# Messages of a graph layer as fp32 rows, with the edges' loop codes as one more column of the product

## The chip, the cores and the metric

The kernel runs on one core of a Trainium2 chip. The metric is the device time of one execution, in microseconds, as the median of several runs. PE is the matmul engine, DVE the vector engine, ACT the scalar engine, POOL and SP the engines that mostly issue DMAs here.

## The reference

A graph has 6,250 nodes with 256 features and 106,250 edges, sorted by destination; each node also has edges to itself (loops). Two layers follow one another, each with a residual and a layer norm. The first one has this core:

```
def edge_nn(x, W, b):
    h = relu(x @ W.T + b)
    return relu(h @ W.T + b)
msgs = zeros
for r in range(2):                       # two kinds of edges
    msgs = where((rel == r)[:, None], edge_nn(feat[src], W_rel[r], b_rel[r]), msgs)
agg = segment_sum(msgs, dst)
gates = agg @ W_ih.T + b_ih + b_hh       # i, f, g, o
c = sigmoid(i) * tanh(g);  hn = sigmoid(o) * tanh(c)
x = relu(hn @ W1.T + b1);  x = relu(x @ W2.T + b2);  return x @ W3.T + b3
```

The second one is a graph attention layer with 4 heads over the same edges: a softmax over the edges that arrive at a node, and a sum of the source rows weighted by it.

## The kernel before

**The start** (`gnn_kernel`, up to L1170). Since a message depends only on the source node and the edge's kind, all 2 x 6,250 messages are computed once per node. For chunks of 4 blocks of 128 nodes, PE makes the hidden layer (`fph`, L1135), ACT its relu (`fhT`, L1142), PE the messages of a block (`fpm`, L1149, a PSUM tile of two buffers). DVE adds the bias (L1158, into `fms`) and ACT takes the relu (L1161). The fp32 message is then split into three bf16 numbers that add up to it, with two ACT casts (L1162, L1164) and two DVE subtractions (L1163, L1165) into `ms3`, and SP stores a block of 384 KB to the table `parts0` in DRAM (L1167): one row of 3 x 256 bf16, 1,536 bytes, for each node and kind.

In the same stretch the chip looks at the edge list. Loops are taken out and the list is compacted: a ladder of shifts on DVE (L885 to L903, into `frame`), 21 indirect scatters by POOL into `packed` (L932), reads back by SP (`both`, L962), then integer work on DVE that gives for each edge its row in `parts0`, its destination, and `mark`, a code that is not zero at the one edge of a node which carries its loops' kinds. The per-edge lists are turned on PE (L1060) so that 128 edges lie on the partitions: 782 tiles of 128 edges. `low_p` (L1077) is PE's first product that needs the list. The order of instructions in this stretch is set by a scheduler, and every engine then runs its queue in order.

**Layer 0** (`fast`). The order is written out by hand, as a loop over the tiles in which `run.step()` advances generators by one step a tile. A group is 14 tiles, whose edges end in at most 128 nodes. For each tile POOL gathers 128 rows of `parts0` (`gather`, L1262) into a buffer `G`, a ring of 10 with 4 tiles each. Four tiles later PE adds the tile to the group's sum with a one-hot matrix of destinations as the weights (`oh0`, made by DVE at L1346 from `iota_s`): a product of 512 columns (L1631, the two upper parts side by side), one of 256 (L1632, the third part), and one of a single column (L1633), which carries `mark` into `codes`, a column of the PSUM tile `bank`. The group's sum `fps0` has two buffers.

When a group is complete, `turn` finishes it: ACT copies the code (L1436), DVE makes two selection matrices from it (`pick`, L1439), PE adds the nodes' own rows `loop0` with four products (L1445, L1446), ACT and DVE fold the two halves (L1450, L1452), PE transposes (L1456) and DVE copies into `faT` (L1459). `update` then takes up to four groups through the gates (L1483) and the small dense layers to `hr` (L1570), the rows of the second layer's table `rows1`. The last groups are taken one at a time; the last of all stores its rows with a POOL scatter (L1579), and only then can the second layer's gathers begin.

**Layer 1** gathers 782 tiles again, from `rows1` (1,040 bytes a row, same helper, same ring, 7 tiles a buffer), weights them on DVE (L1811) and sums them with fp32 products (L1920).

Of the kernel before, what the change touches and what calls it, by code (L numbers as in the profile page):

```python
# [30 lines left out]
F32 = mybir.dt.float32  # L35
I32 = mybir.dt.int32
AF = mybir.ActivationFunctionType
OP = mybir.AluOpType
# [5 lines left out]
P = 128  # L44
N = 6250
D = 256
E = 106250
H = 4
# [6 lines left out]
ZERO0 = 2 * NP  # L55
# [10 lines left out]
BF16 = mybir.dt.bfloat16  # L66
WT = 7
TC = -(-(E - N) // P)
NW = -(-TC // WT)
SLOTS = 64  # L70
NG = NW // 2
CT = 18 * WT
# [4 lines left out]
HA = D + H  # L77
# [627 lines left out]
def gnn_kernel(  # L705
# [26 lines left out]
    nc = tc.nc  # L732
# [6 lines left out]
        return at(ap, 0, [[0, P], [1, n]])  # L739

    dram = ctx.enter_context(tc.tile_pool(name="fdram", bufs=1, space=DRAM))
    parts0 = dram.tile([ZERO0 + 1, 3 * D], BF16, name="parts0")
    rows1 = dram.tile([NP + P, HA], F32, name="rows1")
    slots = dram.tile([NW, (WT + 1) * P], BF16, name="slots")
    cuts = dram.tile([(NC + 1) * CT, P], F32, name="cuts")
# [27 lines left out]
    with (  # L773
# [8 lines left out]
        with nc.allow_non_contiguous_dma(reason="bias vectors, one element a partition"):  # L782
            nc.scalar.dma_start(brc, br.rearrange("r (k p) -> p r k", p=P))
        nc.scalar.dma_start(brr, rows(br, 2 * D))
        zrow = mw.tile([1, 3 * D], BF16, name="fzrow")
        nc.vector.memset(zrow, 0.0)
        nc.sync.dma_start(parts0[ZERO0 : ZERO0 + 1, :], zrow)

        with (
# [260 lines left out]
            for to, of in (  # L1050
                (idx0, row),
                (dstE, list_f[:, :, 1:]),
                (mark, rel_f[:, :, :P]),
                (idx1, src0),
                (first, steps),
            ):
                for k0, kn in blocks_of(NC, 4):
                    pt = lps.tile([P, 4 * CT], F32, name="turned")
                    for k in range(kn):
                        nc.tensor.transpose(  # L1060
                            pt[:, k * CT : (k + 1) * CT], of[:CT, k0 + k, :], ident[:CT, :CT]
                        )
                    n = min(kn * CT, COLS - k0 * CT)
                    nc.vector.tensor_copy(to[:, k0 * CT : k0 * CT + n], pt[:, :n])
            ones = lp.tile([P, P], F32, name="fones")
            nc.vector.memset(ones, 1.0)
            few = lps.tile([P, 4 * CT], F32, name="turned")
# [56 lines left out]
        for b0, bn in blocks_of(NB, CHUNK):  # L1124
            cols = bn * P
            xc = mp.tile([P, 2, CHUNK * P], F32, name="fxc", bufs=3)
            nc.sync.dma_start(
                xc[:, :, :cols], xT[:, b0 * P : b0 * P + cols].rearrange("(k p) n -> p k n", p=P)
            )
            hT = mp.tile([P, 2, 2, CHUNK * P], F32, name="fhT")  # L1130
            for r in range(2):
                for m in range(2):
                    ph = mps.tile([P, CHUNK * P], F32, name="fph")
                    for k in range(2):
                        nc.tensor.matmul(  # L1135
                            ph[:, :cols],
                            WrT_s[:, r, k, m * P : (m + 1) * P],
                            xc[:, k, :cols],
                            start=(k == 0),
                            stop=(k == 1),  # L1140
                        )
                    nc.scalar.activation(  # L1142
                        hT[:, r, m, :cols], ph[:, :cols], AF.Relu, bias=brc[:, r, m : m + 1]
                    )
            for j in range(bn):
                pm = mps.tile([P, 2, D], F32, name="fpm")
                for r in range(2):
                    for k in range(2):
                        nc.tensor.matmul(  # L1149
                            pm[:, r, :],  # L1150
                            hT[:, r, k, j * P : (j + 1) * P],
                            WrT_s[:, r, k, :],
                            start=(k == 0),
                            stop=(k == 1),
                        )
                ms = mp.tile([P, 2, D], F32, name="fms", bufs=3)
                ms3 = mp.tile([P, 2, 3, D], BF16, name="ms3", bufs=3)
                nc.vector.tensor_add(  # L1158
                    ms.rearrange("p r f -> p (r f)"), pm.rearrange("p r f -> p (r f)"), brr
                )  # L1160
                nc.scalar.activation(ms, ms, AF.Relu)  # L1161
                nc.scalar.copy(ms3[:, :, 0, :], ms)  # L1162
                nc.vector.tensor_sub(ms, ms, ms3[:, :, 0, :])  # L1163
                nc.scalar.copy(ms3[:, :, 1, :], ms)  # L1164
                nc.vector.tensor_sub(ms3[:, :, 2, :], ms, ms3[:, :, 1, :])  # L1165
                b = b0 + j
                nc.sync.dma_start(  # L1167
                    parts0[2 * b * P : 2 * (b + 1) * P, :].rearrange("(p r) f -> p (r f)", r=2),
                    ms3.rearrange("p r c f -> p (r c f)"),
                )  # L1170

    odd_v = nc.values_load_multi_w_load_instructions(
# [20 lines left out]
def fast(  # L1193
# [111 lines left out]
    GS = 2 * WT + 1  # L1305
    loops = parts0[: 2 * NP, :].rearrange("(n r) f -> n (r f)", r=2)
    iops = ctx.enter_context(tc.tile_pool(name="iops", bufs=1, space=PSUM))
    bank = iops.tile([P, SLOTS + 4 * GS * H + NG], F32, name="bank")
    iota_s = bank[:, :SLOTS]
    exs = bank[:, SLOTS : SLOTS + 4 * GS * H].rearrange("p (b t h) -> p b t h", b=2, h=H)  # L1310
    codes = bank[:, SLOTS + 4 * GS * H :]
    nc.scalar.copy(iota_s, iota_f[:, :SLOTS])
    keep = ctx.enter_context(tc.tile_pool(name="keep", bufs=1))

# [44 lines left out]
    with (  # L1359
# [37 lines left out]
            zero[: (NP + P - N) // 2, : 2 * HA],  # L1397
        )

        kinds = l0w.tile([P, 2, P], BF16, name="kinds")  # L1400
        for r in range(2):
            nc.vector.tensor_scalar(
                kinds[:, r, :], ident, float(4 - r), 1.0, op0=OP.mult, op1=OP.subtract
            )

        run = Steps()

        def weights_of_logits():
# [21 lines left out]

        def turn(g, i, ps, aT):

            u = everyone
            agg = ring(up, [P, D], F32, "agg", 2)
            code = ring(up, [P, 1], F32, "code", 3)
            nc.scalar.copy(code, codes[:, g : g + 1])  # L1436
            pick = ring(up, [P, 2, P], BF16, "pick", 2)
            for r in range(2):
                nc.vector.tensor_scalar(  # L1439
                    pick[:, r, :], kinds[:, r, :], code, None, op0=OP.is_equal  # L1440
                )
            yield 1
            for r in range(2):
                own = loop0[g][:, 3 * D * r : 3 * D * (r + 1)]
                nc.tensor.matmul(ps, pick[:, r, :], own[:, : 2 * D], start=False, stop=False)  # L1445
                nc.tensor.matmul(  # L1446
                    ps[:, :D], pick[:, r, :], own[:, 2 * D :], start=False, stop=(r == 1)
                )
            yield 1
            nc.scalar.copy(agg[u, :], ps[u, D:])  # L1450
            yield 1
            nc.vector.tensor_add(agg[u, :], agg[u, :], ps[u, :D])  # L1452
            yield 1
            pt = ring(upp, [P, 4 * P], F32, "fpg", 5)[:, : 2 * P]
            for k in range(2):
                nc.tensor.transpose(  # L1456
                    pt[:, k * P : (k + 1) * P], agg[:, k * P : (k + 1) * P], ident
                )
            nc.vector.tensor_copy(  # L1459
                aT[:, :, i * P : (i + 1) * P], pt.rearrange("p (k n) -> p k n", k=2)  # L1460
            )
# [156 lines left out]
        def sum0(g, t, last=False):  # L1618
# [6 lines left out]
                ohj = ohs[g][:, ohj, :]  # L1625
            begins = g not in sums
            if begins:
                sums[g] = ring(eps, [P, 2 * D], F32, "fps0", 2)
            part = got[t]
            ends = last or j == WT - 1  # L1630
            nc.tensor.matmul(sums[g][to, :], ohj, part[:, : 2 * D], start=begins, stop=False)  # L1631
            nc.tensor.matmul(sums[g][to, :D], ohj, part[:, 2 * D :], start=False, stop=False)  # L1632
            nc.tensor.matmul(  # L1633
                codes[to, g : g + 1], ohj, mark[:, t : t + 1], start=begins, stop=ends
            )
            if last:
                quad = next(q for q in quads if g in q)
                if g == quad[0]:
# [7 lines left out]
        for n in range(TC + LAG):  # L1646
            if n < TC:
                g, t = order[n]
                k = n % 4
                if k == 0:  # L1650
                    four = ring(rowsp, [P, WT * HA], F32, "G", 10)[:, : 6 * D]
                    four = four.bitcast(BF16).rearrange("p (j f) -> p j f", j=4)

                got[t] = four[:, 3 - k if n // 40 % 2 else k, :]
                gather(got[t], parts0, idx0[:, t : t + 1])
                if t == order_of(g)[0]:
                    ohs[g] = ring(ep, [P, 2 * W8, SLOTS], BF16, "oh0", 3)
                    one_hot(ohs[g], 2 * g, 2 * W8)
                    loop0[g] = ring(up, [P, 6 * D], BF16, "loop0", 2)
                    own_rows(g, lows_of(windows_of(g)), loop0[g], loops)  # L1660
            if n >= LAG:
                g, t = order[n - LAG]
                if t != 2 * WT * g:
                    sum0(g, t, t == TC - 1)
                elif g:
                    sum0(g - 1, t, True)
                if t == 2 * WT * g + WT:
                    sum0(g, 2 * WT * g)
            run.step()
# [361 lines left out]
```

## Time and profile before

| | us |
|---|---|
| median of 3 runs (2313.48 to 2318.78) | 2316.77 |
| the profiled execution's own time | 2315.23 |
| its span on the core | 2313.5 |
| first gather of layer 0 starts | 231.4 |
| last gather of layer 0 starts | 1219.6 |
| first gather of layer 1 starts | 1261.5 |
| last gather of layer 1 starts | 2246.2 |

| engine | busy us | share of the span |
|---|---|---|
| PE | 1524.3 | 66% |
| DVE | 1276.5 | 55% |
| ACT | 570.3 | 25% |
| POOL | 1529.7 | 66% |

No engine is near 100% over the whole, so the shares alone don't say what sets the time; they are means over stretches with different loads. In the groups of the profile, "busy" is followed by the mean duration of one instruction, and after the bar by the idle time of the engine just before these instructions and what ended most of it. A record of an fp32 matmul is half of one call in the source: the profile shows two for each.

### The profile page before, as it was taken

The numbers are of one execution on the slowest core, as the hardware profiler recorded it, in microseconds if no ns is written. First come the engines' busy times: TensorE is split into PE (matmuls) and PEld (weight loads), VectorE is DVE, ScalarE is ACT, GpSimd is POOL, SyncE is SP. The second block draws the span as 40 slices with busy tenths as digits, with TensorE's granted clock in tenths as the row PEclk, the third lists the DMA queues.
The fourth block names the chain that finished last, engine by engine and source line by source line (L and its number), as shares of the span: only waits on it lengthen the run. The fifth ranks groups of instructions, "written<-read, shape, count | busy, mean of one in ns | idle before, by whom it ended". The sixth has DMA issues, their size and how long they took to land. (4 is left out here: it accounts for less than half of the span.)

```text
span 2313.5 us, 24182 instructions
## 1 busy us (share of the span) xinstructions
PE 1524.3 (66%) x6783; PEld 837.2 (36%) x6783; DVE 1276.5 (55%) x3370; ACT 570.3 (25%) x1623; POOL 1529.7 (66%) x1603
## 2 busy tenths in 40 slices
PE   7888587888887788878985245545455355454554
PEld 4646333443444444444453122223223222232322
DVE  7867222333333333233433377777777778777786
ACT  3647012222222222222343021121211211111211
POOL 1110777777777777777772777777777777777760
PEclk9889588899898999988997667667676676666776
DMA  4333867777877778777873455555555555555550
GB/s 141 135 117 148 221 188 214 209 214 212 230 221 209 212 204 227 223 214 208 228 230 95 133 150 154 148 152 156 148 155 150 148 160 144 156 151 152 150 144 25
DMA packets 175914, 397.68 MB, mean 172 GB/s; under 512 B 42451, under 2 KB 74290, under 8 KB 175769
## 3 DMA queue, kind: packets, MB, share of 16 engines
q0 software_dynamic: 88480, 259.38, 41.8%
q1 hardware_dynamic: 64736, 96.55, 13.1%
q10 hardware_dynamic: 22553, 40.12, 5.7%
q8 instruction: 55, 0.90, 0.2%
q14 instruction: 90, 0.74, 0.1%
HBM read 337.38 MB, written 58.55 MB: 171 GB/s over the span
## 5 line engine op out<-in xcount | busy, mean ns | idle before, releaser
L1262 POOL DMA_INDIRECT G<-parts,fidx x782 | 749.2, 958 | 323.8 <-issue 191.3
L1262 POOL DMA_INDIRECT G<-rows,fidx x782 | 747.7, 956 | 240.2 <-issue 222.7
L1920 PE MATMUL fps<-gw,oh 128*64 128x264 f32 (+1 forms) x1674 | 435.8, 471 | 233.6 <-DVE gw L1811 233.6
L1631 PE MATMUL fps<-G,oh 128*64 128x512 bf16 (+1 forms) x837 | 339.8, 425 | 141.3 <-DMA G<-parts,fidx 126.0
L1920 PEld LDWEIGHTS fps<-gw,oh 128*64 128x64 f32 (+1 forms) x1674 | 229.5, 168 | 409.3 <-DVE gw L1811 248.5
L1811 DVE TENSOR_TENSOR gw<-G,bank 128x1792 f32<-128x1792 f32 (+1 forms) x167 | 249.0, 1491 | 178.5 <-ACT gw L1810 177.7
L1632 PE MATMUL fps<-G,oh 128*64 128x256 bf16 (+1 forms) x837 | 239.5, 295 | 0.0
L1346 DVE TENSOR_TENSOR oh<-bank,fslot 128x1024 bf16<-128x1024 f32 (+1 forms) x112 | 136.6, 1220 | 138.6 <-PE bank L1633 136.2
L1483 PE MATMUL fpg<-faT,fWihT 128*128 128x512 f32 (+2 forms) x432 | 175.5, 533 | 12.1 <-DVE faT L1459 12.1
L1439 DVE TENSOR_SCALAR pick<-kinds,code 128x128 bf16<-128x128 bf16 x112 | 25.2, 281 | 274.8 <-ACT code L1436 274.8
L1633 PE MATMUL bank<-fmark,oh 128*64 128x1 bf16 (+1 forms) x837 | 139.7, 172 | 37.5 <-DVE oh L1346 26.3
L1759 PE MATMUL turn<-fident,e 128*120 128x128 f32 (+2 forms) x30 | 13.7, 457 | 223.3 <-ACT e L1953 223.3
L1631 PEld LDWEIGHTS <-oh 128*64 128x64 bf16 (+1 forms) x837 | 90.1, 113 | 190.2 <-issue 178.1
L1632 PEld LDWEIGHTS <-oh 128*64 128x64 bf16 (+1 forms) x837 | 92.8, 114 | 143.1 <-issue 140.7
L1633 PEld LDWEIGHTS <-oh 128*64 128x64 bf16 (+1 forms) x837 | 96.5, 119 | 105.5 <-issue 33.4
L1860 ACT ACTIVATE frs<-fmv,eps_c 128x1 f32<-128x1 f32 x112 | 33.0, 295 | 302.5 <-DVE fmv L1859 151.8
L1149 PE MATMUL fpm<-fWrT,fhT 128*128 128x256 f32 x392 | 97.3, 405 | 14.4 <-DVE fms L1158 14.4
L1135 PE MATMUL fph<-fxc,fWrT 128*128 128x512 f32 (+1 forms) x208 | 94.2, 599 | 8.1 <-DMA fWrT<-in_WrT_dram 6.5
L932 POOL DMA_INDIRECT packed<-frame,place x21 | 22.8, 1085 | 116.0 <-DVE fms L1163 79.1
L1483 PEld LDWEIGHTS fpg<-faT,fWihT 128*128 128x128 f32 x432 | 72.5, 198 | 72.1 <-issue 48.5
L1866 ACT ACTIVATE fy<-fy,frs 128x256 f32<-128x256 f32 x112 | 67.2, 600 | 100.4 <-DVE gw L1805 53.2
L1149 PEld LDWEIGHTS fpm<-fWrT,fhT 128*128 128x128 f32 x392 | 78.9, 205 | 34.5 <-DVE fms L1158 18.4
(249 smaller groups left out, 2123.0 us busy)
## 6 DMA issues: line engine op xcount, KB each, us to landing
kept<-keep SPq DMA_DIRECT2D x56, 384.0 KB
k<-kept ACTq DMA_DIRECT2D x56, 384.0 KB
loop<-parts SPq DMA_DIRECT2D x110, 192.0 KB
parts<-ms SPq DMA_DIRECT2D x49, 384.0 KB
dB<-slots ACTq DMA_DIRECT2D x112, 128.0 KB
G<-parts,fidx POOLq DMA_INDIRECT x782
G<-rows,fidx POOLq DMA_INDIRECT x782
rows<-hr SPq DMA_DIRECT2D x110, 65.0 KB
```

Source lines behind the costliest of these rows:

```text
L1135: nc.tensor.matmul(ph[:, :cols], WrT_s[:, r, k, m * P : (m + 1) * P], xc[:, k, :cols], start=(k == 0), stop=(k == 1),)
L1149: nc.tensor.matmul(pm[:, r, :], hT[:, r, k, j * P : (j + 1) * P], WrT_s[:, r, k, :], start=(k == 0), stop=(k == 1),)
L1262: nc.gpsimd.indirect_dma_start(out=to_tile, out_offset=None, in_=table, in_offset=bass.IndirectOffsetOnAxis(ap=idx, axis=0),)
L1346: nc.vector.tensor_tensor(to[:, :nj, :], iota_s[:, None, :].to_broadcast([P, nj, SLOTS]), of[:, :, None].to_broadcast([P, nj, SLOTS]), op= ...
L1483: nc.tensor.matmul(pg[:, :cols], WihT_s[:, k, c * P : (c + 1) * P], aT[:, k, :cols], start=(k == 0), stop=(k == 1),)
L1631: nc.tensor.matmul(sums[g][to, :], ohj, part[:, : 2 * D], start=begins, stop=False)
L1632: nc.tensor.matmul(sums[g][to, :D], ohj, part[:, 2 * D :], start=False, stop=False)
L1633: nc.tensor.matmul(codes[to, g : g + 1], ohj, mark[:, t : t + 1], start=begins, stop=ends)
L1811: nc.vector.tensor_mul(gw[:, :, :D].rearrange("p j (h f) -> p j h f", h=H), of[:, :n, :D].rearrange("p j (h f) -> p j h f", h=H), ex[:, o ...
L1860: nc.scalar.activation(r, mv[u, k, 1:2], AF.Ln, bias=eps_c[u])
L1866: nc.scalar.activation(y, y, AF.Identity, bias=m, scale=r)
L1920: nc.tensor.matmul(sums[g][to, :], ohj, gw, start=begins, stop=ends)
```

## The change

The three-part bf16 rows become plain fp32 rows: `parts0` holds 256 fp32 a row (1,024 bytes), the casts and subtractions are gone, and a block's store is 256 KB. In layer 0 a tile is summed by one fp32 product of 257 columns. Its last column is `mark`, which ACT copies into the buffer beside the gathered rows, for 7 tiles at once; for this `mark` is kept in the order of the gathers. `G` holds 7 tiles a buffer, `oh0` is fp32 with two buffers, and `codes` is gone. The own rows are added in `turn` by DVE, with two compares and two multiply-adds.

```
-    parts0 = dram.tile([ZERO0 + 1, 3 * D], BF16, name="parts0")
+    parts0 = dram.tile([ZERO0 + 1, D], F32, name="parts0")
...
-                    nc.vector.tensor_copy(to[:, k0 * CT : k0 * CT + n], pt[:, :n])
+                    if to is not mark:
+                        nc.vector.tensor_copy(to[:, k0 * CT : k0 * CT + n], pt[:, :n])
+                        continue
+
+                    to2, of2 = (
+                        ap.rearrange("p (g j) -> p g j", j=2 * WT)
+                        for ap in (mark[:, k0 * CT : k0 * CT + n], pt[:, :n])
+                    )
+                    for a, b, c in ((0, 1, 0), (1, 2, WT), (2, WT + 1, 1), (WT + 1, 2 * WT, WT + 1)):
+                        nc.vector.tensor_copy(to2[:, :, a:b], of2[:, :, c : c + b - a])
...
                 ms = mp.tile([P, 2, D], F32, name="fms", bufs=3)
-                ms3 = mp.tile([P, 2, 3, D], BF16, name="ms3", bufs=3)
...
                 nc.scalar.activation(ms, ms, AF.Relu)
-                nc.scalar.copy(ms3[:, :, 0, :], ms)
-                nc.vector.tensor_sub(ms, ms, ms3[:, :, 0, :])
-                nc.scalar.copy(ms3[:, :, 1, :], ms)
-                nc.vector.tensor_sub(ms3[:, :, 2, :], ms, ms3[:, :, 1, :])
                 b = b0 + j
                 nc.sync.dma_start(
                     parts0[2 * b * P : 2 * (b + 1) * P, :].rearrange("(p r) f -> p (r f)", r=2),
-                    ms3.rearrange("p r c f -> p (r c f)"),
+                    ms.rearrange("p r f -> p (r f)"),
                 )
...
-    bank = iops.tile([P, SLOTS + 4 * GS * H + NG], F32, name="bank")
+    bank = iops.tile([P, SLOTS + 4 * GS * H], F32, name="bank")
...
-        kinds = l0w.tile([P, 2, P], BF16, name="kinds")
-        for r in range(2):
-            nc.vector.tensor_scalar(
-                kinds[:, r, :], ident, float(4 - r), 1.0, op0=OP.mult, op1=OP.subtract
-            )
...
         def turn(g, i, ps, aT):
-            u = everyone
-            agg = ring(up, [P, D], F32, "agg", 2)
-            code = ring(up, [P, 1], F32, "code", 3)
-            nc.scalar.copy(code, codes[:, g : g + 1])
-            pick = ring(up, [P, 2, P], BF16, "pick", 2)
+            agg = ring(up, [P, D], F32, "agg", 3)
+            kind = ring(up, [P, 2], F32, "kind", 3)
             for r in range(2):
                 nc.vector.tensor_scalar(
-                    pick[:, r, :], kinds[:, r, :], code, None, op0=OP.is_equal
-                )
-            yield 1
-            for r in range(2):
-                own = loop0[g][:, 3 * D * r : 3 * D * (r + 1)]
-                nc.tensor.matmul(ps, pick[:, r, :], own[:, : 2 * D], start=False, stop=False)
-                nc.tensor.matmul(
-                    ps[:, :D], pick[:, r, :], own[:, 2 * D :], start=False, stop=(r == 1)
-                )
-            yield 1
-            nc.scalar.copy(agg[u, :], ps[u, D:])
-            yield 1
-            nc.vector.tensor_add(agg[u, :], agg[u, :], ps[u, :D])
+                    kind[:, r : r + 1], ps[:, D:], float(3 - r), None, op0=OP.is_equal
+                )
+            for r, of in ((0, ps[:, :D]), (1, agg)):
+                nc.vector.scalar_tensor_tensor(
+                    agg,
+                    loop0[g][:, r * D : (r + 1) * D],
+                    kind[:, r : r + 1],
+                    of,
+                    op0=OP.mult,
+                    op1=OP.add,
+                )
             yield 1
...
             if begins:
-                sums[g] = ring(eps, [P, 2 * D], F32, "fps0", 2)
-            part = got[t]
-            ends = last or j == WT - 1
-            nc.tensor.matmul(sums[g][to, :], ohj, part[:, : 2 * D], start=begins, stop=False)
-            nc.tensor.matmul(sums[g][to, :D], ohj, part[:, 2 * D :], start=False, stop=False)
-            nc.tensor.matmul(
-                codes[to, g : g + 1], ohj, mark[:, t : t + 1], start=begins, stop=ends
-            )
+                sums[g] = ring(eps, [P, D + 1], F32, "fps0", 2)
+            ends = last or j in (WT - 1, TC - 1 - 2 * WT * g)
+            nc.tensor.matmul(sums[g][to, :], ohj, got[t], start=begins, stop=ends)
...
-                k = n % 4
+                k, turns = n % WT, n // WT // 10 % 2
                 if k == 0:
-                    four = ring(rowsp, [P, WT * HA], F32, "G", 10)[:, : 6 * D]
-                    four = four.bitcast(BF16).rearrange("p (j f) -> p j f", j=4)
-
-                got[t] = four[:, 3 - k if n // 40 % 2 else k, :]
-                gather(got[t], parts0, idx0[:, t : t + 1])
+                    seven = ring(rowsp, [P, WT * HA], F32, "G", 10).rearrange(
+                        "p (j f) -> p j f", f=HA
+                    )
+                    m = min(WT, TC - n)
+                    of, to = mark[:, n : n + m, None], seven[:, :, D : D + 1]
+                    nc.scalar.copy(to[:, ::-1, :][:, :m, :] if turns else to[:, :m, :], of)
+
+                got[t] = seven[:, WT - 1 - k if turns else k, : D + 1]
+                gather(got[t][:, :D], parts0, idx0[:, t : t + 1])
                 if t == order_of(g)[0]:
-                    ohs[g] = ring(ep, [P, 2 * W8, SLOTS], BF16, "oh0", 3)
+                    ohs[g] = ring(ep, [P, 2 * W8, SLOTS], F32, "oh0", 2)
                     one_hot(ohs[g], 2 * g, 2 * W8)
-                    loop0[g] = ring(up, [P, 6 * D], BF16, "loop0", 2)
+                    loop0[g] = ring(up, [P, 2 * D], F32, "loop0", 2)
```

More of the change, by code (lines that the diff above doesn't have):

```diff
@@ L784, in gnn_kernel @@
         nc.scalar.dma_start(brr, rows(br, 2 * D))
-        zrow = mw.tile([1, 3 * D], BF16, name="fzrow")
+        zrow = mw.tile([1, D], F32, name="fzrow")
         nc.vector.memset(zrow, 0.0)
@@ L1307, in fast @@
     iops = ctx.enter_context(tc.tile_pool(name="iops", bufs=1, space=PSUM))
-    bank = iops.tile([P, SLOTS + 4 * GS * H + NG], F32, name="bank")
+    bank = iops.tile([P, SLOTS + 4 * GS * H], F32, name="bank")
     iota_s = bank[:, :SLOTS]
-    exs = bank[:, SLOTS : SLOTS + 4 * GS * H].rearrange("p (b t h) -> p b t h", b=2, h=H)
-    codes = bank[:, SLOTS + 4 * GS * H :]
+    exs = bank[:, SLOTS:].rearrange("p (b t h) -> p b t h", b=2, h=H)
     nc.scalar.copy(iota_s, iota_f[:, :SLOTS])
```

## The prediction

> **What bounds the kernel now.** I read the windows by stage first, then the instructions of the gather helper L1262, then the timeline of the first 232 us. The windows (length; busy us and count of PE, PEld, DVE, ACT, POOL; clock; DMA share; GB/s):
>
> ```profile
> 0.00:231.40 231.40, 191.11 (x646) 123.62 (x646) 169.81 (x276) 121.26 (x209) 28.96 (x36) 0.92 0.40 135
> 231.40:1219.60 988.20, 795.60 (x3705) 410.37 (x3706) 339.35 (x1113) 235.17 (x580) 749.23 (x783) 0.89 0.77 216
> 1219.60:1261.50 41.90, 27.19 (x130) 18.77 (x129) 13.81 (x60) 20.35 (x49) 2.85 (x3) 0.75 0.20 65
> 1261.50:2246.20 984.70, 481.77 (x2198) 270.34 (x2198) 709.28 (x1801) 180.34 (x739) 746.76 (x782) 0.68 0.55 150
> 2246.20:2313.50 67.30, 28.64 (x106) 14.12 (x104) 44.26 (x122) 13.17 (x48) 1.92 (x2) 0.69 0.13 37
> ```
>
> Layer 0 (second) and layer 1 (fourth) take the same 988 and 985 us with quite different PE, DVE and DMA loads. What they share is POOL:
>
> ```profile
> L1262 POOL DMA_INDIRECT G<-parts,fidx x782: 942/946/1402, 231.4 to 1219.6; - x196
> L1262 POOL DMA_INDIRECT G<-rows,fidx x782: 942/946/1218, 1261.5 to 2246.2; - x196
> ```
>
> Each layer issues 782 gathers, each 0.946 us by the median and 0.30 us of issue after it: 1.25 us a gather, 782 x 1.26 = 985. The rows are 1,536 bytes in layer 0 and 1,040 in layer 1 and the median is equal, so bytes don't set it, nor does PE. Time can only go or come where POOL isn't gathering: before 231.4, between 1219.6 and 1261.5, and after 2246.2, which the change doesn't touch.
>
> In the start, PE (191 of 231 us) waits for two things:
>
> ```profile
> PE fpm L1149 <- DVE fms L1158: 14.4, 4, 6.3
> PE low_p L1077 <- DVE low L981: 10.1, 1, 10.1
> ```
>
> The second ends a chain: the list's compaction on DVE (last step L903), 21 scatters on POOL (L932), the reads back (L962), `low`:
>
> ```profile
> 83.84 1.08 DVE L903 TENSOR_TENSOR frame<-frame,moved 128x896 int32<-128x896 int32 x1
> ...
> 144.56 0.98 POOL L932 DMA_INDIRECT packed<-frame,place  x1 [1.51 <-DMA packed<-frame,place]
> ...
> 156.11 0.77 PE L1077 MATMUL low_p<-low,fones 1*128 1x113 f32 x2 [10.08 <-DVE low L981]
> ```
>
> PE then has 67.5 us of work to 223.6, and the last block ends so:
>
> ```profile
> 223.67 0.69 DVE L1158 TENSOR_TENSOR fms<-fpm,fbrr 128x512 f32<-128x512 f32 x1 [0.61 <-PE fpm L1149]
> 224.28 0.68 DVE L1165 TENSOR_TENSOR ms<-fms,ms 128x512 bf16<-128x512 f32 x1
> 224.39 0.63 ACT L1161 ACTIVATE fms<-fms 128x512 f32<-128x512 f32 x1 [0.68 <-DVE fms L1158]
> 225.05 0.62 ACT L1162 CAST ms<-fms 128x512 bf16<-128x512 f32 x1
> 225.70 0.69 DVE L1163 TENSOR_TENSOR fms<-fms,ms 128x512 f32<-128x512 f32 x1 [0.75 <-ACT ms L1162]
> 226.43 0.62 ACT L1164 CAST ms<-fms 128x512 bf16<-128x512 f32 x1 [0.76 <-DVE fms L1163]
> 227.08 0.69 DVE L1165 TENSOR_TENSOR ms<-fms,ms 128x512 bf16<-128x512 f32 x1 [0.68 <-ACT ms L1164]
> ```
>
> Its store and POOL's waits take the 3.6 us to the first gather at 231.36.
>
> [...] the trace has 684 (L1158) and 0.42 us (L1452)[...] in layer 1, 12 fp32 products of 264 columns issue back to back in 5.33 us, 0.444 each, and one tile's three bf16 products (769 columns) are 0.36 apart (starts 1216.39, 1216.75, 1217.11). [...] the column above goes from 0.89 to 0.68 where PE is busy half the time.
>
> **The change, part by part.**
>
> *Splits of the messages (49 blocks).* Gone: 98 DVE subtractions and 98 ACT casts, 67 and 60 us busy; a subtraction takes 0.60 us of DVE's queue (start to start). In this part the scheduler fixes each engine's order when the program is built. Counting DVE's instructions to L903: before, 11 adds L1158 and 20 subtractions; in the changed program's order, 17 adds and no subtraction. That is 20 x 0.60 - 6 x 0.60 = 8.4, plus an idle 0.7: L903 ends **9.1 us earlier**, at 76.7. I went through the adds: PE has each block ready in time, since with fewer DVE instructions between the adds its two PSUM buffers come free. The scatters (61 us) and the reads (9.2) follow unchanged, so `low` comes at 147.
>
> *PE's order.* The scheduler now puts 74 products L1135 and 144 L1149 (source calls; each is two records) ahead of `low_p`, where it had 66 and 128. At 0.86 and 0.4355 us (16 records in 7.03, 32 in 7.07) the moved 8 and 16 are 6.9 + 7.0 = **13.9 us** that go from after `low` to before it. There is room: the earlier part had 15.5 us of idle and 8 us of slow L1149 bursts while DVE was behind. PE's work to `low_p` is 74 x 0.86 + 144 x 0.4355 = 126.4 from 6.5, with 3 for the cold start: about 136, so it still waits 11 us, which absorbs errors here.
>
> *The last block* loses casts and subtractions: 225.02 to 227.77, **2.75 us**. *mark in gather order*: 8 small copies for 2 on DVE after the reads, **+0.5**, on PE's way to the next transposes.
>
> Added wait: `fms` is now what is stored, so an add waits until the store of three blocks ago has landed; behind it in DVE's queue is the compaction. Add 0.7, activation 0.7, issue 0.4, landing some 2.5 (227.77 to 230.4 at the end) are 4.3; three blocks of PE are 5.2. Cost 0, at worst a microsecond in a few places (+5). SP's queue keeps stores, loads of `fxc` and the reads back in the same sequence. Stores and gathers move a third less; nothing waits for those bytes.
>
> First gather: 231.4 - 9.1 - 13.9 - 2.75 + 0.5 = **206.1**.
>
> *Layer 0's sums.* Per product 0.36 becomes 0.44 for 257 columns; x837: +70 us of PE. The four loop products a group (L1445, L1446: some 0.7) go: -40. In their place two 128x1 compares (0.16 each) and two multiply-adds (0.42) on DVE, 1.2 a group, for two `pick` (0.56) and an add (0.42); ACT loses two copies. The transposes now stand one product after the group's last sum, so PE waits some 1.2 us for DVE there, the next group's products behind it; before it waited 1.75 at L1483 for `faT`. ACT gains 112 column copies at some 0.2 (as L1961) = 22 us of 988; PE's first product of seven waits for one that was queued 4 gathers before. The gathers get no wait on ACT, and their waits on PE (102 for 209) are on tiles 70 back. `oh0` in fp32 with two buffers: still 1.22 from PSUM, and its 136 us of waiting for L1633 go. All this is under POOL's 988 us, at **0**: PE would be busy 795.6 - 301 (837 x 0.36) - 40 + 372 (837 x 0.444) = 827 of 988. If that cover fails, see the rivals.
>
> *End of layer 0.* The last sum ends at 1232.6; `code`, `pick`, four products, copy, add, transposes and `faT` run to 1238.04, 5.4 us. The new chain is 0.3 + 0.85 + 0.65 + 0.4, with hand-overs 2.6: **-2.8**, bounds 0 (the previous group's chain on ACT is then last) and -7 (the backlog of 11 products at 1219.6 drains sooner without the `bank` waits). Layer 1 is as before, shifted.
>
> **Sum.** -25.2 - 2.8 = -28.0. The profiled execution took 2315.23 (span 2313.5), so 2287.2; the median of the runs was 1.5 above it: **2288.5**.
>
> **Rivals.** *(a) The start keeps its length in part*: the adds wait for stores or PE, so L903 isn't earlier (2298), or DVE's work after the reads, not PE, paces what follows, and the 13.9 is lost as well (2311). For it: DVE is full from 18 to 85 us. Against: its instructions there fall by 14. Chance 0.20, a quarter of it within 0.2%. *(b) Slower: PE becomes layer 0's bound.* 827 us are at a clock of 0.89; at layer 1's 0.68 they are 827 x 0.89/0.68 = 1082, 94 over POOL's 988: 2382. It decides from a clock under 0.745. For it: fp32 products in layer 1 ran at 0.68. Against: there they come in bursts behind DVE, here one every 1.25 us, and a PE that falls behind is a busy one. 0.07. *(c) The bytes do matter* and a gather gets shorter: 0.01, unbounded below; the equal medians speak against it. *(d) No effect at all*, if PE's work alone sets the start: 2316.8; the waits shown speak against it (inside (a)).
>
> **Numbers.** The main case has 0.72: 2288.5, its own range 2279 to 2297. With the better part of (a) and the bounds above, 2277 to 2305. A measurement tells about 0.2% (4.6 us) from no change. Faster 0.88, same 0.05, slower 0.07.
>
> **What would show it.** First gather near 206; L932's first near 77; `low_p` waiting about 11 us at 147; no wait of `fpm` products on the adds over 2 us before that; gathers at 0.946 and 1.25 apart with 988 us; PE clock of layer 0 above 0.8; 38 to 40 us between the layers. A first gather after 220, or gathers further apart than 1.27, would prove it wrong.

## The result, and the profile after

The kernel after takes **2276.5 us** (median of 4 runs, 2273.88 to 2276.94) against 2316.03 for the kernel before beside it (4 runs): a ratio of 0.9827, with a 95% interval of 0.9810 to 0.9844. The profiled execution of after took 2273.88 us, with a span of 2271.7. The time lies 12 us under the forecast and 0.5 us under the low end of the range. Ratios, here and below, compare fast runs with fast runs and need not equal the quotient of the two medians in the last digits.

The windows of the kernel after, cut at the same events as before (length; busy us and count of PE, PEld, DVE, ACT, POOL; clock; DMA share; GB/s):

```profile
0.00:203.70 203.70, 181.13 (x646) 118.63 (x646) 110.79 (x184) 68.84 (x121) 26.98 (x35) 0.97 0.38 122
203.70:1190.40 986.70, 838.64 (x2702) 353.93 (x2703) 361.53 (x1177) 229.06 (x581) 748.48 (x783) 0.93 0.54 157
1190.40:1221.00 30.60, 16.49 (x75) 10.95 (x73) 11.13 (x50) 15.20 (x38) 2.92 (x4) 0.78 0.19 65
1221.00:2205.10 984.10, 484.51 (x2198) 271.61 (x2198) 708.83 (x1804) 180.86 (x739) 746.23 (x781) 0.68 0.55 151
2205.10:2271.70 66.60, 29.57 (x104) 14.56 (x104) 43.23 (x119) 12.94 (x47) 2.06 (x2) 0.65 0.13 37
```

| stretch | before | after | change | forecast |
|---|---|---|---|---|
| start, to the first gather of layer 0 | 231.4 | 203.7 | -27.7 | -25.2 |
| gathers of layer 0, first to last start | 988.2 | 986.7 | -1.5 | 0 |
| gap, to the first gather of layer 1 | 41.9 | 30.6 | **-11.3** | **-2.8** |
| gathers of layer 1 | 984.7 | 984.1 | -0.6 | 0 |
| end | 67.3 | 66.6 | -0.7 | 0 |

Three stretches came as worked out. The start is within 2.5 us. The two long stretches don't move, though PE has 43 us more to do in layer 0 and a third of the gathered bytes is gone (the DMA share falls from 0.77 to 0.54). The gap is where the forecast failed. What a gather costs is the same in the gathers' lines of after:

```profile
L1265 POOL DMA_INDIRECT G<-parts,fidx x782: 942/946/1431, 203.7 to 1190.4; - x196
L1265 POOL DMA_INDIRECT G<-rows,fidx x782: 942/946/1207, 1221.0 to 2205.1; - x196
```

The timeline of after around the gap (start, us, engine, line, tiles; in brackets the idle time before, and who ended it):

```profile
1190.38 0.95 POOL L1265 DMA_INDIRECT G<-parts,fidx  x1 [0.30 <-issue]
...
1193.23 1.26 PE L1622 MATMUL fps<-G,oh 128*64 128x257 f32 x4
...
1194.53 0.22 DVE L1433 TENSOR_SCALAR kind<-fps 128x1 f32<-128x1 f32 x2 [1.71 <-PE fps L1622]
...
1220.96 0.96 POOL L1265 DMA_INDIRECT G<-rows,fidx  x1 [2.69 <-issue]
```

The last sum of layer 0 ends at 1194.49, 4.1 us after the last gather starts; in the kernel before it ended at 1232.65, 13.1 us after. That is -9.0. From the last sum to the first gather of layer 1 the two take 28.8 and 26.5: -2.3 (parts are cut to tenths so that they add up to the table's). So the shorter chain behind the last sum, for which I forecast -2.8, is right, and what I missed is **the backlog**: the sums that PE still owes when the gathers are done.

What made PE late is seen in its waits. When PE has caught up with POOL, it waits for the next gathered rows. In the kernel before it does that for the last time at 1085.1, ahead of the 720th of the 837 calls in which layer 0's gathered rows are summed; from there on it is behind. Its six largest waits from that call to the end of the last sum (who waited <- for whom: us in total, times, longest):

```profile
PE fpg L1483 <- DVE faT L1459: 5.1, 6, 1.5
PE fps L1445 <- DVE pick L1439: 4.3, 1, 4.3
PE bank L1633 <- ACT code L1436: 2.9, 7, 1.3
PE fpg L1507 <- DVE fhn L1503: 2.4, 2, 1.2
PE fps L1631 <- DMA G<-parts,fidx: 2.4, 1, 2.4
PE bank L1633 <- DVE oh L1346: 1.8, 2, 1.6
```

All waits of the kernel after, from the same call (1055.7) to the end of the last sum:

```profile
PE fps L1622 <- DMA G<-parts,fidx: 4.8, 4, 2.5
PE fpg L1499 <- DVE fhn L1495: 1.8, 2, 1.0
PE fpg L1448 <- DVE agg L1437: 1.3, 2, 0.7
PE fpg L1545 <- DVE keep L1536: 0.3, 1, 0.3
```

The wait for rows in the first list, and 0.2 us of that in the second, lie ahead of the call. From its start, before needs 147.5 us to the end of the last sum: 129.9 of work and 17.4 of waits for DVE and ACT. After needs 138.8: 130.7 of work, 3.4 of waits for DVE, and 4.5 of waits for rows. The last gather starts 134.4 and 134.7 us after that call. So PE's own work is the same within a microsecond (the sums are dearer, the loop products are gone), and 14.0 us of waits for other engines are gone. PE catches up with the gathers again, so not all of the 14.0 is won: the backlog is 9.0 shorter, and 4.5 become waits for rows.

### The profile page after: what moved, and what is told of

The parts are those of the page before. It is cut to its first block, busy times and chain, and to the rows that moved or that the text cites. A ratio compares the mean times of both kernels' runs of the same rounds, so it can differ in the third digit from the quotient of the medians.

```text
span 2271.7 us, 22029 instructions
## 1 busy us (share of the span) xinstructions
PE 1550.3 (68%) x5722; PEld 769.7 (34%) x5722; DVE 1235.5 (54%) x3332; ACT 506.9 (22%) x1525; POOL 1526.7 (67%) x1603
## 5 line engine op out<-in xcount | busy, mean ns | idle before, releaser
L1265 POOL DMA_INDIRECT G<-parts,fidx x782 | 748.5, 957 | 305.7 <-issue 218.4
L1622 PE MATMUL fps<-G,oh 128*64 128x257 f32 (+1 forms) x1674 | 523.4, 425 | 149.2 <-DMA G<-parts,fidx 142.4
L1622 PEld LDWEIGHTS fps<-G,oh 128*64 128x64 f32 (+1 forms) x1674 | 191.9, 147 | 457.4 <-DMA G<-parts,fidx 241.5
L1433 DVE TENSOR_SCALAR kind<-fps 128x1 f32<-128x1 f32 x112 | 12.5, 152 | 308.5 <-PE fps L1622 308.5
L1348 DVE TENSOR_TENSOR oh<-bank,fslot 128x1024 f32<-128x1024 f32 x112 | 135.9, 1213 | 2.2 <-ACT bank L1781 2.2
L1583 DVE COPY nd<-hr 128x4 f32<-128x4 f32 x56 | 10.9, 194 | 162.6 <-ACT hr L1562 162.6
L1157 PE MATMUL fpm<-fWrT,fhT 128*128 128x256 f32 x392 | 89.0, 380 | 0.6 <-DVE fms L1165 0.5
L1750 PEld LDWEIGHTS turn<-fident,e 128*120 128x120 f32 (+2 forms) x30 | 5.0, 168 | 238.0 <-ACT e L1944 236.0
L1801 ACT COPY gw<-bank 128x28 f32<-128x28 f32 (+1 forms) x167 | 28.4, 170 | 228.5 <-DMA dB<-slots 101.3
L1157 PEld LDWEIGHTS fpm<-fWrT,fhT 128*128 128x128 f32 x392 | 73.3, 190 | 17.7 <-issue 5.0
L1165 DVE TENSOR_TENSOR fms<-fpm,fbrr 128x512 f32<-128x512 f32 x49 | 33.6, 687 | 76.1 <-PE fpm L1157 74.9
```

What stands on the lines that cost most here:

```text
L1157: nc.tensor.matmul(pm[:, r, :], hT[:, r, k, j * P : (j + 1) * P], WrT_s[:, r, k, :], start=(k == 0), stop=(k == 1),)
L1165: nc.vector.tensor_add(ms.rearrange("p r f -> p (r f)"), pm.rearrange("p r f -> p (r f)"), brr)
L1265: nc.gpsimd.indirect_dma_start(out=to_tile, out_offset=None, in_=table, in_offset=bass.IndirectOffsetOnAxis(ap=idx, axis=0),)
L1348: nc.vector.tensor_tensor(to[:, :nj, :], iota_s[:, None, :].to_broadcast([P, nj, SLOTS]), of[:, :, None].to_broadcast([P, nj, SLOTS]), op= ...
L1622: nc.tensor.matmul(sums[g][to, :], ohj, got[t], start=begins, stop=ends)
L1801: nc.scalar.copy(gw[:, :, D:HA], ex[:, o : o + n, :])
```

## The experiments

Theory 1: the PSUM tile `bank` is the cause. DVE's comparison (L1346) reads the slot numbers in it while PE writes `codes` into it for every tile (L1633); each waits for the other (in layer 0 of before DVE 136.2 us for L1633, PE 26.3 us for L1346). Theory 2: `turn` is, whose four steps come so late that its transposes stand next to the gates. Theory 3: the number of PE's products is. Beside these, the working of the start was to be tested. Where lines are given, those of a kernel with an edit may be shifted by a few from the kernel that it comes from.

The first four kernels ran on another chip, on which the kernel before takes 3087.3 us: in the profile there of the kernel with the slot numbers in SBUF (below), the gathers of layer 0 stand 1.57 us and those of layer 1 1.89 us apart in the mean, and such stalls hide the gap. From these, only the start, which ends before the gathers, can be read.

**The splits put back into the start of after, into a scratch tile.**

```
                 nc.scalar.activation(ms, ms, AF.Relu)
+                ms3 = mp.tile([P, 2, 3, D], BF16, name="ms3", bufs=3)
+                nc.scalar.copy(ms3[:, :, 0, :], ms)
+                nc.vector.tensor_sub(ms3[:, :, 1, :], ms, ms3[:, :, 0, :])
+                nc.scalar.copy(ms3[:, :, 2, :], ms3[:, :, 1, :])
+                nc.vector.tensor_sub(ms3[:, :, 0, :], ms3[:, :, 1, :], ms3[:, :, 2, :])
```

> The kernel after, with two casts on ACT and two subtractions on DVE of 128x512 put back for each of the 49 blocks, into a scratch tile that nothing reads; the store still waits for the activation alone. My theory of the start (the subtractions stand in DVE's queue ahead of the list's compaction, and the built order then puts fewer of PE's products ahead of low_p): first scatter at about 86 instead of 77.6, and, as 69 products L1143 and 128 L1157 are now built ahead of low_p against 74 and 144, 5 x 0.86 + 16 x 0.4355 = 11.3 us more after it: first gather at 203.7 + 9 + 11 = 224, time about 2296. Rival (the third fewer bytes stored, or a higher PE clock, made the start short): first gather at 208 at the most, time under 2281. The gap between the layers stays at 30 to 31 in either.

The first gather starts at 224.2, as expected; the bytes stored are those of after, so the rival of the bytes falls. The clock doesn't explain it either: from `low_p` to the first gather it is 0.94 in both. (The time, 3070.57 us, ratio to before 0.9949 with 0.9933 to 0.9965, carries that chip's gathers.) PE's waits in the start of this kernel:

```profile
PE low_p L1085 <- DVE low L980: 12.3, 1, 12.3
PE fpm L1157 <- DVE fms L1165: 12.2, 4, 5.5
```

The wait for DVE's add, 0.5 us in after, is back at 12.2. `low_p` runs at 154.17 instead of 146.18 (+8.0), and from there to the first gather it is 70.0 instead of 57.5 (+12.5, expected 11.3). One term is off in its place: the first scatter came 4.4 us later (82.0), not 8, and the 21 scatters took 60.9 us instead of 57.3. So the sum came out partly by luck; that the splits are the cause, and the bytes are not, doesn't hang on it.

**The slot numbers in SBUF (kernel before).**

```
-    iota_s = bank[:, :SLOTS]
+    iota_s = iota_f[:, :SLOTS]
...
-    nc.scalar.copy(iota_s, iota_f[:, :SLOTS])
```

> The kernel before, with the 64 slot numbers that one_hot compares read from SBUF instead of from the PSUM tile `bank`; the codes stay in `bank`. Theory 1 (the tile `bank`, written by PE's product L1633 for every tile of edges and read by DVE's comparison L1346 for every group, holds DVE, and through DVE's queue the turn of a group, and through that PE; so PE is 11 products late at the last gather): the comparison's 138.6 us of idle before it fall under 20, the backlog at the last gather falls from 13.1 us to about 5, the gap between the layers from 41.9 to about 33, the time by about 9 us to 2307. Theory 2 (the longer chain of turn, with its four products, copies and four steps, makes the backlog) and theory 3 (the smaller number of products a tile makes it drain faster) expect a gap of 41 to 42 and no change of the time by more than 2 us.

On the first chip: 3081.56 us, ratio 0.9979 (0.9963 to 0.9994), the last sum 24.3 us behind the last gather. That says nothing of the three theories. The same edit on a chip with gathers 1.26 us apart:

> The same edit of the kernel before as in e1_iota_sbuf (slot numbers read from SBUF, codes left in `bank`), run again because that chip's gathers stood 1.57 and 1.89 us apart and hid the stretch in question. Where the gathers are 1.26 us apart, theory 1 (the shared tile `bank`) expects the comparison's idle of 138.6 us to fall under 20, the last sum to end about 5 us after the last gather's start instead of 13.1, the gap between the layers to fall from 41.9 to about 33, the time by 7 to 10 us. Theories 2 (the longer chain of turn) and 3 (fewer products a tile) expect a gap of 41 to 42 and a change under 2 us.

It took 2346.92 us against 2313.87, a ratio of **1.0141** (1.0123 to 1.0158): slower, which no theory had. The comparison's wait is gone, the last sum comes 7.8 us behind the last gather, the gap is 35.7. But both layers' gathers take longer: 1012.7 us (+24.5) and 1011.9 (+27.2); the end of the kernel, 53.9 us instead of 67.3, gives a part back. The gathers of this kernel, with the longest at 2.2 us, and the timeline where one meets the comparison:

```profile
L1262 POOL DMA_INDIRECT G<-parts,fidx x782: 942/947/2205, 232.3 to 1245.0; - x196
```

```profile
610.36 0.95 POOL L1262 DMA_INDIRECT G<-parts,fidx  x1 [0.30 <-DMA G<-parts,fidx]
611.43 1.22 DVE L1345 TENSOR_TENSOR oh<-fiota,fslot 128x1024 bf16<-128x1024 f32 x1
611.61 1.86 POOL L1262 DMA_INDIRECT G<-parts,fidx  x1 [0.30 <-issue]
613.77 0.95 POOL L1262 DMA_INDIRECT G<-parts,fidx  x1 [0.30 <-issue]
```

The comparison ends at 612.65, the gather 0.82 us later: it took 0.91 us longer than the next one, and ran beside the comparison for 1.04 us. Of the 98 gathers of layer 0 that overlap a comparison in this trace, 59 took over 1.0 us; in the kernel before, whose comparison takes one input from PSUM, 10 of 91 did. The comparison itself is as long in both (1.22 us). Why gathers take longer beside it when both its inputs are in SBUF isn't shown. The edit had moved more than the wait, and the slower gathers alone gave PE time to catch up, so the 7.8 is no clean answer.

**The codes in a bank of their own (kernel before)**, which leaves the comparison's inputs as they are; the ring `fpg` gets 4 buffers in all its places.

```
-    bank = iops.tile([P, SLOTS + 4 * GS * H + NG], F32, name="bank")
+    bank = iops.tile([P, SLOTS + 4 * GS * H], F32, name="bank")
...
-    codes = bank[:, SLOTS + 4 * GS * H :]
...
+        codes = upp.tile([P, NG], F32, name="codes")
...
-                    pg = ring(upp, [P, 4 * P], F32, "fpg", 5)
+                    pg = ring(upp, [P, 4 * P], F32, "fpg", 4)
```

> The kernel before, with the codes in a PSUM tile of their own, in a bank taken from the ring fpg (4 buffers instead of 5); the slot numbers stay in PSUM, so that DVE's comparison reads what it read before. Theory 1 (the shared tile) expects the comparison's 136 us of waiting for L1633 to go, the last sum to end 7 to 9 us after the last gather's start instead of 13.1, as in the run with the slot numbers in SBUF (7.8), but with the gathers 1.26 us apart and layer 0's gathers at 988 us, and so a gap near 36 and a time 5 to 6 us shorter. If that run's 7.8 came only from its slower gathers, the last sum stays at 12 to 14 us and the gap at 41 to 43. If four buffers of fpg are too few, the products of the updates wait for DVE or ACT and the gap grows.

2314.35 us against 2316.96: 0.9990 (0.9982 to 0.9998). The last sum comes 9.8 us behind the last gather (13.1 before), the gap is 37.6 (-4.3), and layer 0's gathers take 991.0, +2.8: POOL is busy 752.7 us there, 749.2 before, and 51 of the gathers take over 1.0 us, 36 before. The comparison no longer waits for PE. This is less than theory 1 had (7 to 9 us, a gap near 36) and more than nothing: it accounts for some 3.3 of the 9.0 us. PE's largest waits from the 720th call (1089.1) to the end of the last sum show what is left:

```profile
PE fpg L1483 <- DVE faT L1459: 5.2, 6, 1.5
PE fps L1445 <- DVE pick L1439: 2.7, 1, 2.7
...
PE codes L1633 <- ACT code L1436: 2.7, 7, 1.1
```

The wait for the comparison (`oh`, 1.8 us) is gone and that for `pick` is 1.6 us shorter; the waits for `faT` and `code` are about as they were.

**A late turn (kernel after).**

```
         def turn(g, i, ps, aT):
+            yield 3
             agg = ring(up, [P, D], F32, "agg", 3)
```

> The kernel after, with three more steps of waiting at the head of turn, so that the two comparisons, multiply-adds and the transposes come four products after a group's last sum, as before, and the sums' buffer stays taken as long. Theory 2 expects the gap between the layers to go from 30.6 back to 36 or more and the time up by 5 to 9 us. Theories 1 and 3 expect a gap of 30 to 32 and a change of the time under 2 us.

On the first chip: ratio 1.0 (0.9976 to 1.0023), gap 50.4; inconclusive. Again where the gathers are 1.26 us apart:

> The same edit of the kernel after as in e2_late_turn (three more steps ahead of turn's comparisons), run again for the same reason. Theory 2 expects the gap between the layers to go from 30.6 to 36 or more and the time up by 5 to 9 us; theories 1 and 3 a gap of 30 to 32 and a change under 2 us.

2287.55 us against 2313.87, a ratio of 0.9887 (0.9870 to 0.9904): of the 40 us won, 13 are lost. The last sum comes 7.9 us behind the last gather, +3.8, though the chain behind it was a little shorter in this execution (25.4); the gap is 33.3, +2.7. PE's largest waits from the 720th call (1064.9) to the end of the last sum are of the kind that before had:

```profile
PE fpg L1449 <- DVE agg L1438: 4.3, 4, 1.3
PE fpg L1476 <- DVE faT L1452: 3.2, 6, 0.6
```

`update` issues its first gates four steps after the last sum of a quad (the groups that it takes together). A turn of four steps puts the transposes into that same step, and PE waits there for `agg` and then for `faT` (4.3 and 3.2 us in this list). In after the transposes come one step after the sum, and three tiles' products lie between them and the gates. So theory 2 holds too, for some 3.8 us (the waits grow by 6.5, PE's own work by 2.1, and 4.5 of waits for rows are used up). The larger part of the 13 us, 8.9, is in layer 0's gathers (995.6), by as much as POOL is busy longer (757.3 against 748.5), with gathers of up to 1.69 us; nothing in the forecast of either theory had that. Where these long gathers stand is shown in the last section.

**The coupling put back (kernel after), and the same product without it.** One more product of one column a tile, into `bank`, which has its columns of codes again:

```
+            nc.tensor.matmul(
+                codes[to, g : g + 1], ohj, got[t][:, D:], start=begins, stop=ends
+            )
```

> The kernel after, with one more product a tile, of one column, which writes the codes a second time into a part of the PSUM tile `bank`, as before; nothing reads it. The slot numbers stay in `bank`. Theory 1 expects the comparison L1348 to wait for PE again (over 100 us in layer 0), the backlog at the last gather back at 10 us or more, the gap between the layers at 37 to 40 against 30.6, the time up by 6 to 10 us. Theory 2 expects a gap of 30 to 32 and under 2 us; theory 3 (fewer products) some 2 to 4 us from the product's own time in the backlog.

On the first chip: 3106.44 us, 1.0050 (1.0031 to 1.0068), gap 54.9; inconclusive. Again:

> The same edit of the kernel after as in e4_coupled_again (one more product a tile, of one column, into a part of `bank`), run again for the same reason. Theory 1 expects the comparison L1348 to wait for PE over 100 us again, the last sum 10 us or more behind the last gather, the gap at 37 to 40 against 30.6, the time up by 6 to 10 us. Theory 2 expects a gap of 30 to 32. Theory 3 expects 2 to 4 us from the product's own time. If PE, with about 100 us more work, is itself too full, the gathers stand further apart than 1.27 us, and the run tells nothing of the three.

2282.26 us against 2313.87: 0.9856 (0.9837 to 0.9874). The comparison L1349 waits for PE again (169.4 us), the last sum is 9.4 us behind the last gather, the gap 34.9. This is less than theory 1 had. Its control adds the product into the group's own sums, so that `bank` is untouched:

```
-            nc.tensor.matmul(sums[g][to, :], ohj, got[t], start=begins, stop=ends)
+            nc.tensor.matmul(sums[g][to, :], ohj, got[t], start=begins, stop=False)
+            nc.tensor.matmul(
+                sums[g][to, D:], ohj, got[t][:, D:], start=False, stop=ends
+            )
```

> The kernel after, with the same extra one-column product a tile as in f4_coupled_again, but added into the group's own sums (the code counts twice, and turn compares with doubled values), so that `bank` is untouched. If the 5.3 us by which that run's last sum came later are PE's extra work (some 54 us in layer 0), they come here as well: last sum 9 us after the last gather, gap 34 to 35. If they are the waits on the shared tile (theory 1), the last sum ends 4 to 6 us after the last gather, the gap is 30 to 32, and the comparison L1348 waits under 20 us.

2277.01 us against 2316.96: 0.9837 (0.9819 to 0.9855). The comparison waits for PE no longer (2.7 us in the whole run, for ACT), yet the last sum is 7.4 us behind the last gather, +3.3, and the gap 34.0. So most of the effect of the coupled product in after is PE's work (two records of 0.19 us a call); the other 2.0 us, the difference of two single executions, may be the coupling. Neither of the two expectations was met: the truth lay between.

**Both at once (kernel after).**

> The kernel after, with both edits: three more steps ahead of turn's comparisons, and the one-column product into `bank`. The late turn alone put the last sum 3.8 us later behind the last gather (7.9 instead of 4.1), the coupled product alone 5.3 (9.4). If they are two separate causes of the 9 us, they add: last sum at 13, the 13.1 of the kernel before, gap 38 to 39. If they are one cause twice, it stays at 9 to 10, gap 34 to 36.

2294.73 us against 2316.96: 0.9898 (0.9880 to 0.9916). The last sum is 13.6 us behind the last gather, as if the two effects added. The gap is 41.3, more than the 38 to 39 expected since its chain was longer (27.7). Layer 0's gathers take 998.6; here the gather of the last group's own rows waits 7.2 us, by the trace for DVE.

**A version of after with the last group's update first.**

```
+            first = groups[-1] == NG - 1
-            yield 4
+            yield 1 if first else 4
...
-                    yield (slow + 1) // 2
+                    if not first:
+                        yield (slow + 1) // 2
...
-            yield slow - 1
+            if not first:
+                yield slow - 1
```

> The kernel after, with the update of the last group of layer 0 put ahead of the rest of the one before it: its gates, all six in one step, come one step after its start instead of four, and its tanh with them. In the trace of after, PE stands behind the other group's products until 1199.1 though faT is ready at 1196.74 (2.3 us), and the table of the square root is loaded between the last group's gates, and theirs loaded again (2 x 1.28 us). If the chain of the last group sets the gap, both go: gap 30.6 to about 26, time down by 4 to 5 us to 2272. If the other group's chain is as late, the gap stays above 29.

2273.97 us against 2313.87: 0.9828 (0.9812 to 0.9845), not to be told from after. The chain behind the last sum is 23.5 us, 3.0 shorter: the gates run at 1197.53, and two of the three table loads (ACT_TABLE_LOAD, 1.28 us each) are gone. But the last sum came 5.6 us behind the last gather instead of 4.1, though the order of instructions up to it isn't changed: PE's own work from the 720th call on was 133.5 us instead of 130.7. So one execution's backlog can differ from another's by 1.5 us at least. The gap is 29.1, 1.5 shorter, not 4 to 5.

The gap's two parts in the profiles of these chips (one execution each), with PE's waits for DVE and ACT and its own work from the 720th call to the end of the last sum:

| kernel | layer 0's gathers | last sum, behind last gather | chain to layer 1 | gap | PE's waits | PE's work |
|---|---|---|---|---|---|---|
| before | 988.2 | 13.1 | 28.8 | 41.9 | 17.4 | 129.9 |
| before, slot numbers in SBUF | 1012.7 | 7.8 | 27.9 | 35.7 | 14.5 | 128.4 |
| before, codes in their own bank | 991.0 | 9.8 | 27.8 | 37.6 | 14.4 | 128.2 |
| after | 986.7 | 4.1 | 26.5 | 30.6 | 3.4 | 130.7 |
| after, late turn | 995.6 | 7.9 | 25.4 | 33.3 | 9.9 | 132.8 |
| after, coupled product | 989.4 | 9.4 | 25.5 | 34.9 | 2.7 | 140.1 |
| after, uncoupled product | 985.6 | 7.4 | 26.6 | 34.0 | 1.6 | 140.0 |
| after, late turn and coupled product | 998.6 | 13.6 | 27.7 | 41.3 | 9.3 | 146.0 |
| after, last group first | 985.2 | 5.6 | 23.5 | 29.1 | 3.1 | 133.5 |

The chain varies by a microsecond or two between kernels in which it is the same code, and the backlog by 1.5, so differences of that size aren't read. Theory 3 in its plain form falls: the change leaves PE's work in this stretch as it was. That more work would have made it later is shown by the two kernels with an extra product.

## Why the prediction was right, and where it failed

- *What bounds the kernel*: right. POOL's gathers hold 988 and 985 us of both kernels, and time came only from outside them.
- *The start*: right in its mechanism, -27.7 for -25.2. L903's counterpart ended at 76.67, forecast 76.7; but in before it ended at 84.92, so it moved by 8.25 us and not by the 9.1 of my count, and the two figures of the forecast don't fit each other. Part of that was made up by luck: the scatters took 57.3 us from first to last start instead of 58.7. `low_p` waited 10.8 us (forecast 11) and ran at 146.18 (147); the wait of `fpm` fell from 14.4 to 0.5 us. The splits put back returned 20.5 us. The forecast's 3 us "for the cold start" are as in the trace of before, where the first 16 records of L1135 took 9.89 us and 16 later ones 7.03; with the granted clock at 1.00 in these 9.89 us, why isn't shown. Of the 2.5 us missed, 0.8 are `low_p`'s and 1.6 PE's work after it (57.5 us for 59.1); over the whole start its clock was 0.97 for 0.92. One reading was wrong at little cost: the first gather does wait for ACT, which makes ten column copies ahead of it (1.08 us).
- *Rival (a)* is out with the first scatter, *(b)* with the clock: layer 0 ran at 0.93, for 0.89 before, and PE was busy 839 us (forecast 827). That a busier PE is granted a higher clock was my estimate from the windows (0.68 in layer 1, where PE is busy for 49%), and isn't shown as a rule: with the uncoupled product it was busy 898 us at 0.91. *(c)* is out with the median gather of 946 ns at two thirds of the bytes.
- *Layer 0's sums at 0*: right for the 988 us, and it is the step that misled. I wrote that PE's waits for `faT` and DVE's waits for L1633 all lie under POOL's gathers. For PE that cover ends where it last catches up with the gathers, at 1085.1, 134 us ahead of the last one. By the source, that is about where groups are no longer taken by four: the last eight go in pairs, then singly. From there on, what PE waits for another engine it owes at the end.
- *End of layer 0*, the step that failed: -2.8 with bounds 0 and -7; it was **-11.3**. The chain's term was right, -2.3. The backlog's term was wrong: it stood at nothing in the sum and only at an end of the range, and with only one cause, the waits on `bank`. It measured -9.0, since 14.0 us of PE's waits went with the change. Undoing the coupling in before is worth some 3.3 us; the late turn in after costs some 3.8. The 1.9 us between them and 9.0 aren't separated and are near what single executions differ by: in between lie the four loop products and the wait for `pick`, which go with them, and the dearer sums. That both edits to after together give 13.6 isn't proof of the same sum, since the product that I added there is dearer than the one that the change took away.
- A slip in the sum: 2287.2 and 1.5 are 2288.7, not 2288.5.

The span fell by 41.8 us instead of 28.0. Of the 13.8 more, 9.0 are the backlog, 2.5 the start, 2.1 the two long stretches and 0.7 the end; the chain gave 0.5 less.

## What to carry to other kernels

Work that is hidden under a bound engine is uncovered where that engine's stage ends. So price the drain, what another engine still owes when the bound one is done, by itself: find where the draining engine last waits for the bound one, list who else it waits for from there on, and sum what the change does to these waits, instead of leaving them at nothing because the stage's total hides them. And when a wait is to be taken away in an experiment, keep the operands where they are: moving the slot numbers to SBUF took away 136 us of waiting and cost 33 us of time.

## What the runs showed of the hardware

- A gather, 0.95 us by the median, took 1.86 us beside a comparison of 1.22 us with both inputs in SBUF. Beside such comparisons 59 of 98 gathers took over 1.0 us; beside those with one input in PSUM, 10 of 91. In the late turn, long gathers stand beside the addition of `fbias` to `keep`, both in SBUF, which runs there for several groups in a row:

```profile
754.90 1.42 DVE L1552 TENSOR_TENSOR keep<-keep,fbias 128x256 f32<-128x256 f32 x4
755.45 1.69 POOL L1265 DMA_INDIRECT G<-parts,fidx  x1 [0.30 <-issue]
```

What the gathers of layer 0 take beyond 946 ns each is 17.6 us in all in that run, 8.7 in after. If each long gather is put down to the DVE instruction that overlaps it longest, this addition has 7.6 of it (1.1 in after), and the two multiply-adds of the new `turn` 2.1 (0.8). So a change of DVE's timing, with no instruction added, went with 8.9 us more in POOL's gathers.

- On one of the chips the same program took 3087 us instead of 2316, with the same 0.95 us a gather and the same start (229.9 for the kernel before's start, with the slot numbers in SBUF), but with stalls between the gathers. What causes them stays open.
